# Nine of 32 rows of a graph convolution gathered by GpSimd between the packs of the other 23

## The chip, the core and the metric

The kernel runs on one NeuronCore of a Trainium2 chip. Its engines work side by side, each through its own stream of instructions in order: PE (TensorE, matrix products, with weight loads shown apart as PEld), DVE (VectorE), ACT (ScalarE), POOL (GpSimd, here the engine that issues gathers by index) and SP (SyncE, here only an issuer of plain DMAs). The metric is the device time of one execution in microseconds, as the median of several runs. Beside it there is one profiled execution, whose time is longer and whose rows carry the durations used below.

## What is computed

A graph has 12,500 nodes with 16 features each and 412,500 weighted edges, sorted by destination. Two stages follow each other. The first is a pair of graph convolutions, the second a mesh network with two message-passing steps over the same edges (64 features per edge), which the change does not touch. Each convolution does this:

```python
deg = segment_sum(ew, c)
dis = where(deg > 0, rsqrt(deg), 0)
norm = dis[r] * ew * dis[c]
msg = (x @ W.T)[r] * norm[:, None]
out = segment_sum(msg, c) + b
```

Here `r` is an edge's source and `c` its destination. So each edge fetches a row of 16 numbers by its source, multiplies it by a weight, and adds it into its destination. In the kernel the weight that is left at this place is `ew` alone: `dis` is multiplied into the table before and into the sums after, and the self-loops are put in when the table is made.

## The kernel before

**Rows.** The edges are cut into 128 rows of 3,223 (padded to `RL` = 3,328) in order of destination, so that a row covers fewer than `LR` = 112 destinations. A sort at the start (L204 to 361) orders each row by source. The key is source times 128 plus the destination's distance from the row's first node. From the sorted key come, for each edge, `mod` (the source modulo 256, bf16, written to HBM as `mod_d`), `slot_t` (which block of 256 sources, counted from the first of its tile's window), `drel_t` (the destination within the row) and `ew_t` (the weight). The last three are turned by PE (L347) so that 128 edges lie on the partitions and (tile, row) on the free axis. There are `NS` = 26 tiles of 128 edges in a row.

**The loop.** `messages` (L552) runs once per convolution. It makes the table of 12,500 rows of 16 numbers (`fill`), writes it to HBM (L558, L559), and holds it in SBUF as three bf16 parts `t3` whose sum is the fp32 value (`parts3`, L366). Then a hardware loop of `NR // RI` = 4 turns follows, with `RI` = 32 rows unrolled in each. All engines meet at the end of a turn. In a turn, for each row `r`:

- `load` (L575) has SP broadcast the row's `mod` to all partitions, 832 KB, one row ahead.
- `half_row` (L579) has DVE compare half of `mod` with the partition's number and with that number plus 128: two bf16 instructions of 1,664 elements, so four for a row. They are the one-hots `roh` that choose sources.
- `begin` (L587) has DVE make `wm`, the weight put at its slot, in two instructions, and takes a PSUM bank.
- `select` (L597) takes a pack of 4 or 5 tiles; a row has six packs. PE multiplies each tile's one-hots with `t3`, six bf16 matmuls a tile (three parts times two halves of 256), into a bank. DVE makes the one-hots of the destinations `ohd` (L611), then reads the bank times `wm` into `msg` (L614).
- `add_up` (L620) has PE sum `msg` over the pack's edges by `ohd`, in fp32, one pack behind; at a row's last pack ACT copies the sums out (L629).
- `fold_up` (L632) has PE sum the slots' sixteens (L635), and DVE adds the result to `agg` at the row's first node (L639).

**What sets the order.** The loop's code names no order beyond that of its text. A planner in the compiler's front end (the tile scheduler) lays every engine's stream out at build time. It walks a model of the machine with its own prices, and whenever an engine is free in that model it places an instruction that is ready there, the earliest of the text first. An instruction is ready when its inputs are done and its output has a buffer; each name of a tile has so many buffers (`bufs`, two if nothing is said; `roh`, `ohd` and `msg` have three). On the chip each engine then runs its stream strictly in that order and waits at semaphores. The later edge stage is different: there the streams of PE, DVE and ACT are kept in the text's order (`manual_schedule`), and POOL gathers eight times 128 rows of 64 numbers for each group of 1,024 edges (L415).

Of the kernel before, what the change touches and what calls it, by code (L numbers as in the profile page):

```python
# [29 lines left out]
SIGMAS = 4.5  # L30
LR = 112
RI = 32
EPS = 1e-5
MAGIC = 1597463007.0

# [2 lines left out]
def gcn_then_mesh_gnn_kernel(ctx: ExitStack, tc: tile.TileContext, a: dict, out: bass.AP):  # L38
# [86 lines left out]
    def bank(name):  # L125
        return psum.tile([128, 512], F32, name=f"ps_{name}")
# [77 lines left out]

    srt = ExitStack()
    so = srt.enter_context(tc.tile_pool(name="sorted", bufs=1))
    slot_t = so.tile([P, NS, NR], F32, name="slot_t")
    drel_t = so.tile([P, NS, NR], F32, name="drel_t")
    ew_t = so.tile([P, NS, NR], F32, name="ew_t")
    with tc.tile_pool(name="sort", bufs=1) as sp, \  # L210
            tc.tile_pool(name="psort", bufs=1, space=bass.MemoryType.PSUM) as pp:
        keys = [sp.tile([NR, RL], F32, name=f"key{i}") for i in range(2)]
# [90 lines left out]

        nc.vector.tensor_copy(ki, k)

        mod = sp.tile([NR, RL], BF16, name="mod")
        nc.vector.tensor_scalar(kj, ki, 7, 255, op0=OP.arith_shift_right, op1=OP.bitwise_and)
        nc.vector.tensor_copy(mod, kj)
# [31 lines left out]
        nc.vector.tensor_copy(k, ki)  # L340
        nc.sync.dma_start(rstat_d, st)
        for t, to in ((free, slot_t), (k, drel_t), (vals[turn], ew_t)):
            for j0 in range(0, NS, 4):
                n = min(4, NS - j0)
                pt = pp.tile([128, 512], F32, name="ps_st", bufs=2)
                for j in range(n):
                    nc.tensor.transpose(pt[:, j * NR:(j + 1) * NR], tiles(t)[:, j0 + j, :], ident)  # L347
                nc.scalar.copy(to[:, j0:j0 + n, :], pt[:, :n * NR].rearrange("e (j r) -> e j r", r=NR))
        rstat = sp.tile([1, 3, NR], F32, name="rstat")
        for i in range(3):  # L350
            nc.sync.dma_start(rstat[:, i, :], rstat_d[:, i:i + 1].rearrange("r o -> o r"))
# [153 lines left out]
    with tc.tile_pool(name="gcn", bufs=1) as gp, tc.tile_pool(name="gcnw", bufs=2) as gw:  # L505
# [7 lines left out]
            nc.sync.dma_start(fold[b * F:(b + 1) * F, :], ident[0:F, 0:F])  # L513
        iof = gp.tile([128, 2], F32, name="iof")
        nc.gpsimd.iota(iof, pattern=[[128, 2]], base=0, channel_multiplier=1, allow_small_or_imprecise_dtypes=True)
        ior = gp.tile([P, LR], F32, name="ior")
        nc.gpsimd.iota(ior, pattern=[[1, LR]], base=0, channel_multiplier=0, allow_small_or_imprecise_dtypes=True)
        xn = gp.tile([NP, NB, F], F32, name="xn")
        full, wide = N // P, 4 * P
        nwide = -(-N // wide)  # L520
# [31 lines left out]
        def messages(table, fill):  # L552
# [10 lines left out]
            with tc.tile_pool(name="rows", bufs=2) as rw:  # L563
                with tc.For_i(0, trip_count(2, NR // RI)) as it:
                    bases = rw.tile([1, RI], I32, name="rbases")
                    nc.vector.tensor_copy(bases, rbase_row[0:1, ds(it * RI, RI)])
                    mine = []
                    for t, name in ((slot_t, "rslot"), (drel_t, "rdrel"), (ew_t, "rew")):
                        c = rw.tile([P, NS, RI], F32, name=name, bufs=1)
                        nc.vector.tensor_copy(c, t[:, :, ds(it * RI, RI)])  # L570
                        mine.append(c)
                    slot, drel, ew = mine
                    rows, loaded, sums, folds = {}, {}, [], []

                    def load(r):  # L575
                        loaded[r] = rw.tile([128, RL], BF16, name="mod")
                        nc.sync.dma_start(loaded[r], mod_d[ds(it * RI + r, 1), :].to_broadcast([128, RL]))

                    def half_row(r, h):  # L579

                        oh = rw.tile([128, 2, RL // 2], BF16, name="roh", bufs=3)
                        for i in range(2):
                            nc.vector.tensor_scalar(oh[:, i, :], loaded[r][:, h * (RL // 2):(h + 1) * (RL // 2)],  # L583
                                                    iof[:, i:i + 1], None, op0=OP.is_equal)
                        return oh

                    def begin(r):  # L587
                        wm = rw.tile([P, NS, SB], F32, name="wm")
                        nc.vector.tensor_tensor(wm, iow[:, None, :SB].to_broadcast([P, NS, SB]),
                                                slot[:, :, r:r + 1].to_broadcast([P, NS, SB]), op=OP.is_equal)  # L590
                        nc.vector.tensor_tensor(wm, wm, ew[:, :, r:r + 1].to_broadcast([P, NS, SB]), op=OP.mult)
                        ohs = [None, None]
                        h = packs[0][0] // (NS // 2)
                        ohs[h] = half_row(r, h)
                        rows[r] = ohs, wm, bank("seg")

                    def select(r, j0, n, sb):  # L597
                        ohs, wm, acc = rows[r]
                        pg = bank("h")
                        for j in range(j0, j0 + n):  # L600
                            h, at = divmod(j, NS // 2)
                            if ohs[h] is None:
                                ohs[h] = half_row(r, h)
# [7 lines left out]
                        nc.vector.tensor_tensor(ohd[:, :n, :], ior[:, None, :].to_broadcast([P, n, LR]),  # L611
                                                drel[:, j0:j0 + n, r:r + 1].to_broadcast([P, n, LR]), op=OP.is_equal)
                        msg = rw.tile([P, 512], F32, name="msg", bufs=3)
                        nc.vector.tensor_tensor(  # L614
                            msg[:, :n * sb * F].rearrange("p (j s f) -> p j s f", s=sb, f=F),
                            pg[:, :n * sb * F].rearrange("p (j s f) -> p j s f", s=sb, f=F),
                            wm[:, j0:j0 + n, :sb, None].to_broadcast([P, n, sb, F]), op=OP.mult)
                        return r, j0, n, sb, ohd, msg

                    def add_up(r, j0, n, sb, ohd, msg):  # L620
                        acc = rows[r][2]
                        for j in range(n):
                            nc.tensor.matmul(acc[:sb * F, :LR], msg[:, j * sb * F:(j + 1) * sb * F],  # L623
                                             ohd[:, j, :], start=(j0 + j == packs[0][0]),
                                             stop=((j0, n, sb) == packs[-1] and j == n - 1))
                        if (j0, n, sb) == packs[-1]:
                            m = packs[0][2] * F
                            sl = rw.tile([SB * F, LR], F32, name="sl")
                            nc.scalar.copy(sl[:m], acc[:m, :LR])  # L629
                            folds.append((r, sl))  # L630

                    def fold_up(r, sl):  # L632
                        tot = bank("t")
                        m = packs[0][2] * F
                        nc.tensor.matmul(tot[:F, :LR], fold[:m], sl[:m], start=True, stop=True)  # L635
                        at = nc.values_load(bases[0:1, r:r + 1], engines=[ET.DVE], min_val=0, max_val=N,
                                            skip_runtime_bounds_check_because="a destination is a node's number or N")
                        w = agg[:, ds(at, LR)]
                        nc.vector.tensor_add(w, w, tot[:F, :LR])  # L639

                    load(0)
                    for r in range(RI):
                        if r + 1 < RI:
                            load(r + 1)
                        begin(r)
                        for i, pack in enumerate(packs):
                            sums.append(select(r, *pack))
                            if len(sums) > 1:
                                add_up(*sums.pop(0))
                            if folds and i >= 2:  # L650
                                fold_up(*folds.pop(0))
                    add_up(*sums.pop(0))
                    fold_up(*folds.pop(0))

        def spread_degrees():
            with tc.tile_pool(name="spread", bufs=2) as sw:
# [656 lines left out]
```

## Time and profile before

| | us |
|---|---|
| median of three runs (13,435.96 to 13,443.75) | 13,442.51 |
| the profiled execution | 15,403.32 |
| its span, first to last instruction | 15,401.6 |
| the first convolution's loop, four turns | 1,299 to 3,003 |
| the second convolution's loop, four turns | 3,131 to 4,836 |
| the two edge steps | about 5,120 to 15,350 |

The profile's page gives each engine's busy time, then the span cut into 40 slices of 385 us with the busy share of each engine in tenths. A second kind of view gives the busy time of each engine in a stretch. A third lists instructions in order of time with their duration and, in brackets, the idle time before them and what ended it. A fourth gives, for one tile, each instruction's shortest, median and longest duration in nanoseconds. Page groups that bear on the loop: PE at L607 (39,936 selecting matmuls) and L623 (13,312 records), DVE at L611, L614 and L583, and no POOL work at all.

### The profile page before, as it was taken

What the parts mean: (1) busy time and instruction counts of PE and PEld (TensorE: products, weight loads), DVE (VectorE), ACT (ScalarE), POOL (GpSimd) and SP (SyncE); (2) the same over time, 40 slices, a digit from 0 to 9 for tenths busy, and PEclk for the clock granted to TensorE, in tenths of its full rate; (3) what the DMA queues carried; (4) which work ended last, traced back from release to release, by engine and by line L of the source; (5) the groups of instructions that cost most, each with busy time, mean ns of one, the idle gap of its engine ahead of it and who ended that gap; (6) DMA issues with size and microseconds to landing.
All of it is one profiled execution on the core that took longest, in us unless ns stands there. A gap on an engine that the chain in (4) does not pass through costs nothing. (4 is left out here: it accounts for less than half of the span.)

```text
span 15401.6 us, 272960 instructions
## 1 busy us (share of the span) xinstructions
PE 11359.6 (74%) x104538; PEld 8563.0 (56%) x104539; DVE 8752.5 (57%) x22373; ACT 2374.3 (15%) x3731; POOL 6386.7 (41%) x6741
## 2 busy tenths in 40 slices
PE   0089999999998788888888888875666666666665
PEld 0078999889997455555555555553444444444443
DVE  9977777677777455455555555553444444444444
ACT  3400000000000222222222222221111111111111
POOL 0000000000001555556556665555666666666665
PEclk9999999999997688788888888886777777777777
DMA  0001111111111222222222222222222222222222
GB/s 29 0 15 54 66 64 66 50 67 66 65 65 47 56 59 59 58 60 62 59 59 62 59 62 60 60 60 59 61 60 60 61 60 60 61 60 60 61 59 50
DMA packets 958543, 871.49 MB, mean 57 GB/s; under 512 B 599416, under 2 KB 706192, under 8 KB 956548
## 3 DMA queue, kind: packets, MB, share of 16 engines
q1 hardware_dynamic: 258034, 493.54, 9.5%
q0 software_dynamic: 207360, 212.75, 6.8%
q10 hardware_dynamic: 491796, 147.08, 4.1%
q8 instruction: 859, 14.07, 0.4%
q14 instruction: 494, 4.05, 0.1%
HBM read 718.12 MB, written 134.51 MB: 55 GB/s over the span
## 5 line engine op out<-in xcount | busy, mean ns | idle before, releaser
L415 POOL DMA_INDIRECT pg<-tab_p,si x6480 | 6293.6, 971 | 3901.1 <-issue 1707.5
L1052 PE MATMUL ps_o<-eb_w,h 128*128 128x128 f32 x6480 | 1389.3, 381 | 1822.1 <-ACT h L1045 1623.5
L1052 PEld LDWEIGHTS ps_o<-eb_w,h 128*128 128x128 f32 x6480 | 1184.3, 274 | 2078.7 <-ACT h L1045 1762.4
L607 PE MATMUL ps_h<-t,roh 128*128 128x112 bf16 (+1 forms) x39936 | 2131.9, 211 | 65.9 <-DVE roh L583 65.9
L607 PEld LDWEIGHTS <-roh 128*128 128x128 bf16 x39936 | 2011.2, 98 | 115.3 <-issue 112.0
L789 POOL MEMSET zero<- 64x192 bf16 x1 | 0.3, 252 | 4015.1 <-DVE agg L639 4015.1
L1116 DVE TENSOR_SCALAR ot<-rb,iop 128x512 bf16<-128x512 bf16 x810 | 295.5, 365 | 2349.4 <-DMA rb<-relg_d 1482.8
L623 PE MATMUL ps_seg<-ohd,msg 128*112 128x112 f32 (+1 forms) x13312 | 1618.5, 266 | 0.0
L474 DVE TENSOR_REDUCE var<-sq 128x8 f32<-128x512 f32 (+2 forms) x1290 | 843.1, 666 | 1291.8 <-issue 743.9
L397 PE MATMUL ps_seg<-oh,y 128*64 128x64 f32 x19440 | 1298.7, 255 | 208.6 <-issue 197.9
L623 PEld LDWEIGHTS ps_seg<-ohd,msg 128*112 128x112 f32 (+1 forms) x13312 | 1407.4, 172 | 0.5
L397 PEld LDWEIGHTS ps_seg<-oh,y 128*64 128x64 f32 x19440 | 1141.8, 166 | 370.3 <-issue 348.0
L1040 PE MATMUL ps_h<-e,eb_w 128*128 128x512 f32 x1620 | 1193.3, 820 | 64.2 <-issue 36.4
L614 DVE TENSOR_TENSOR msg<-ps_h,wm 128x448 f32<-128x448 f32 (+1 forms) x1536 | 975.0, 635 | 460.5 <-PE ps_h L607 455.0
L611 DVE TENSOR_TENSOR ohd<-ior,rdrel 128x448 f32<-128x448 f32 (+1 forms) x1536 | 1011.1, 659 | 235.3 <-PE ps_seg L623 235.3
L473 ACT ACTIVATE sq<-ps_o 128x512 f32<-128x512 f32 (+1 forms) x1240 | 735.4, 593 | 2587.6 <-remote 668.8
L1045 ACT ACTIVATE h<-ps_h,eb_b 128x512 f32<-128x512 f32 x810 | 556.7, 687 | 3047.7 <-remote 2019.4
L1040 PE MATMUL ps_h<-ot,qd 128*128 128x512 bf16 x2430 | 784.4, 424 | 110.1 <-issue 97.3
L479 DVE TENSOR_TENSOR y<-ps_o,rs_y 128x512 f32<-128x512 f32 x1215 | 802.8, 688 | 88.1 <-issue 4.6
L385 DVE TENSOR_TENSOR oh<-iow,drl 128x512 f32<-128x512 f32 x1215 | 830.0, 683 | 14.4 <-DMA drl<-rel_d 7.2
L1042 PE MATMUL ps_h<-ident,pg 128*128 128x128 f32 x3240 | 603.1, 296 | 309.9 <-issue 236.5
L1052 PE MATMUL ps_o<-ee_w,h 128*128 128x128 f32 x3240 | 626.6, 353 | 238.5 <-ACT h L1033 232.8
(280 smaller groups left out, 11483.2 us busy)
## 6 DMA issues: line engine op xcount, KB each, us to landing
mod<-mod_d SPq DMA_DIRECT2D x256, 832.0 KB
pg<-tab_p,si POOLq DMA_INDIRECT x6480
e_d<-e SPq DMA_DIRECT2D x405, 256.0 KB
e<-e_d SPq DMA_DIRECT2D x405, 256.0 KB
rb<-relg_d ACTq DMA_DIRECT2D x1612, 64.0 KB
qd<-tab_q ACTq DMA_DIRECT2D x1612, 24.0 KB
at<-in_attrT SPq DMA_DIRECT2D x405, 32.0 KB
tab_q<-tabs SPq DMA_DIRECT2D x50, 187.5 KB
```

What stands on the lines that cost most here:

```text
L385: nc.vector.tensor_tensor(oh, iow[:, None, :].to_broadcast([P, K, W]), drl[:, g * K:(g + 1) * K, None].to_broadcast([P, K, W]), op=OP.is_e ...
L397: nc.tensor.matmul(ps[r:r + n, :W], v, oh[:, k, :], start=(k == 0), stop=(k == K - 1))
L415: nc.gpsimd.indirect_dma_start(out=to[:, k, :], out_offset=None, in_=table, in_offset=bass.IndirectOffsetOnAxis(ap=idx[:, k:k + 1], axis=0))
L473: nc.scalar.activation(sq, o.rearrange("p (k f) -> p k f", f=D), AF.Square, scale=D ** -0.5)
L474: nc.vector.tensor_reduce(v[:, i:i + k], sq, axis=AX.X, op=OP.add)
L479: nc.vector.tensor_tensor(y, o, r[:, i:i + k, None].to_broadcast(list(y.shape)), op=OP.mult)
L607: nc.tensor.matmul(pg[:, (j - j0) * sb * F:(j - j0 + 1) * sb * F], ohs[h][:, u, at * P:(at + 1) * P], t3[:, i, u, b:b + sb * F], start=(i ...
L611: nc.vector.tensor_tensor(ohd[:, :n, :], ior[:, None, :].to_broadcast([P, n, LR]), drel[:, j0:j0 + n, r:r + 1].to_broadcast([P, n, LR]), o ...
L614: nc.vector.tensor_tensor(msg[:, :n * sb * F].rearrange("p (j s f) -> p j s f", s=sb, f=F), pg[:, :n * sb * F].rearrange("p (j s f) -> p j ...
L623: nc.tensor.matmul(acc[:sb * F, :LR], msg[:, j * sb * F:(j + 1) * sb * F], ohd[:, j, :], start=(j0 + j == packs[0][0]), stop=((j0, n, sb) ...
L1040: nc.tensor.matmul(ph, w, v, start=(i == 0), stop=False)
L1052: nc.tensor.matmul(po[:, j * 128:(j + 1) * 128], h[:, j * P:(j + 1) * P], w1, start=False, stop=(j == KP - 1))
```

## The change

`GR = range(3, 28, 3)` names nine of the 32 rows of a turn. These rows no longer go through `load`, `half_row`, `begin`, `select`, `add_up` and `fold_up`. For each of them POOL fetches the 16 features of every edge's source from the table in HBM, 26 gathers of 128 rows (`fetch`, into `xg`, three buffers). DVE multiplies them by the weights and splits them into three bf16 parts `x3` (two buffers). DVE then makes one-hots of the destinations in bf16 for five tiles at a time (`goh`, two buffers), and PE sums each tile with one matmul of 48 columns, all 26 into one bank. ACT copies the bank, PE turns and adds the three parts with three small fp32 matmuls, and DVE adds the result to `agg`. The work of such a row is cut into ten pieces by a generator, and one piece is written behind each pack of the 23 other rows. The sources' numbers are kept for this as `src_t`, turned like the other three after the sort. `slot_t` and `drel_t` become bf16.

```diff
+GR = range(3, 28, 3)
...
-    slot_t = so.tile([P, NS, NR], F32, name="slot_t")
-    drel_t = so.tile([P, NS, NR], F32, name="drel_t")
+    slot_t = so.tile([P, NS, NR], BF16, name="slot_t")
+    drel_t = so.tile([P, NS, NR], BF16, name="drel_t")
+    src_t = so.tile([P, NS, NR // RI * len(GR)], I32, name="src_t")
...
+        nc.vector.tensor_single_scalar(kj, ki, 7, op=OP.arith_shift_right)
+        nc.vector.tensor_copy(vals[1 - turn], kj)
+        srcf = sp.tile([P, NS, NR // RI, len(GR)], F32, name="srcf")
+        turned_tiles(vals[1 - turn], lambda j0, n, v: nc.scalar.copy(
+            srcf[:, j0:j0 + n], v.rearrange("e j (i r) -> e j i r", r=RI)[:, :, :, GR.start:GR.stop:GR.step]))
+        nc.vector.tensor_copy(src_t, srcf.rearrange("e j i r -> e j (i r)"))
...
+                    srci = rw.tile([P, NS, len(GR)], I32, name="rsrc", bufs=1)
+                    nc.vector.tensor_copy(srci, src_t[:, :, ds(it * len(GR), len(GR))])
...
+                    def fetch(i):
+                        xg = rw.tile([P, NS, F], F32, name="xg", bufs=3)
+                        for j in range(NS):
+                            nc.gpsimd.indirect_dma_start(
+                                out=xg[:, j, :], out_offset=None, in_=table,
+                                in_offset=bass.IndirectOffsetOnAxis(ap=srci[:, j, i:i + 1], axis=0))
+                        return xg
+                    def gathered(i, xg):
+                        r = GR[i]
+                        x3 = rw.tile([P, NS, 3, F], BF16, name="x3")
+                        acc = bank("o")
+                        def weigh_row():
+                            nc.vector.tensor_tensor(xg, xg, ew[:, :, r:r + 1].to_broadcast([P, NS, F]), op=OP.mult)
+                        def split():
+                            parts3(rw, "x3", xg, [x3[:, :, k, :] for k in range(3)])
+                        def some(j0):
+                            n = min(5, NS - j0)
+                            oh = rw.tile([P, 5, P], BF16, name="goh")
+                            nc.vector.tensor_tensor(oh[:, :n, :], ior[:, None, :].to_broadcast([P, n, P]),
+                                                    drel[:, j0:j0 + n, r:r + 1].to_broadcast([P, n, P]), op=OP.is_equal)
+                            return lambda: [nc.tensor.matmul(
+                                acc[:, :3 * F], oh[:, j, :], x3[:, j0 + j].rearrange("p k f -> p (k f)"),
+                                start=(j0 + j == 0), stop=(j0 + j == NS - 1)) for j in range(n)]
...
+                        def turn(sl):
+                            tot = bank("t")
+                            for k in range(3):
+                                nc.tensor.matmul(tot[:F, :P], sl[:, k * F:(k + 1) * F], ident, start=(k == 0), stop=(k == 2))
...
+                            nc.vector.tensor_add(w, w, tot[:F, :LR])
+                        yield weigh_row()
+                        yield split()
+                        due = None
+                        for j0 in range(0, NS, 5):
+                            after = some(j0)
+                            if due:
+                                due()
+                            due = after
+                            yield
+                        due()
+                        sl = end()
+                        yield
+                        turn(sl)
+                    others = [r for r in range(RI) if r not in GR]
+                    due = {min(3 + (i * (len(others) - 3)) // (len(GR) - 1), len(others) - 1): i for i in range(len(GR))}
+                    fetched = {i: fetch(i) for i in range(2)}
+                    pieces = []
...
-                    load(0)
-                    for r in range(RI):
-                        if r + 1 < RI:
-                            load(r + 1)
+                    load(others[0])
+                    for m, r in enumerate(others):
+                        if m + 1 < len(others):
+                            load(others[m + 1])
+                        if m in due:
+                            i = due[m]
+                            pieces.append(gathered(i, fetched.pop(i)))
+                            if i + 2 < len(GR):
+                                fetched[i + 2] = fetch(i + 2)
                         begin(r)
                         for i, pack in enumerate(packs):
                             sums.append(select(r, *pack))
...
+                            piece()
                     add_up(*sums.pop(0))
                     fold_up(*folds.pop(0))
+                    while pieces:
+                        piece()
```

The gathered rows are thus written at the 4th, 6th, 9th, 11th, 14th, 16th, 19th, 21st and 23rd of the 23 other rows (`due` maps 3, 5, 8, 10, 13, 15, 18, 20, 22 to the gathered rows 0 to 8).

More of the change, by code (lines that the diff above doesn't have):

```diff
@@ L304, in gcn_then_mesh_gnn_kernel, with turned_tiles @@
         nc.vector.tensor_copy(ki, k)
+        def turned_tiles(t, put):
+            for j0 in range(0, NS, 4):
+                n = min(4, NS - j0)
+                pt = pp.tile([128, 512], F32, name="ps_st", bufs=2)
+                for j in range(n):
+                    nc.tensor.transpose(pt[:, j * NR:(j + 1) * NR], tiles(t)[:, j0 + j, :], ident)
+                put(j0, n, pt[:, :n * NR].rearrange("e (j r) -> e j r", r=NR))
+        nc.vector.tensor_single_scalar(kj, ki, 7, op=OP.arith_shift_right)
[4 more added lines that the diff above has]
+        nc.vector.tensor_copy(src_t, srcf.rearrange("e j i r -> e j (i r)"))
         mod = sp.tile([NR, RL], BF16, name="mod")
@@ L342, in gcn_then_mesh_gnn_kernel @@
         for t, to in ((free, slot_t), (k, drel_t), (vals[turn], ew_t)):
[L343 to L348, printed above, removed]
+            turned_tiles(t, lambda j0, n, v: nc.scalar.copy(to[:, j0:j0 + n, :], v))
         rstat = sp.tile([1, 3, NR], F32, name="rstat")
@@ L515, in gcn_then_mesh_gnn_kernel @@
         nc.gpsimd.iota(iof, pattern=[[128, 2]], base=0, channel_multiplier=1, allow_small_or_imprecise_dtypes=True)
-        ior = gp.tile([P, LR], F32, name="ior")
-        nc.gpsimd.iota(ior, pattern=[[1, LR]], base=0, channel_multiplier=0, allow_small_or_imprecise_dtypes=True)
+        ior = gp.tile([P, P], F32, name="ior")
+        nc.gpsimd.iota(ior, pattern=[[1, P]], base=0, channel_multiplier=0, allow_small_or_imprecise_dtypes=True)
         xn = gp.tile([NP, NB, F], F32, name="xn")
@@ L610, in select @@
                         ohd = rw.tile([P, 5, LR], F32, name="ohd", bufs=3)
-                        nc.vector.tensor_tensor(ohd[:, :n, :], ior[:, None, :].to_broadcast([P, n, LR]),
+                        nc.vector.tensor_tensor(ohd[:, :n, :], ior[:, None, :LR].to_broadcast([P, n, LR]),
                                                 drel[:, j0:j0 + n, r:r + 1].to_broadcast([P, n, LR]), op=OP.is_equal)
@@ new lines, in gathered, with end @@
+                    def gathered(i, xg):
[14 more added lines that the diff above has]
+                                start=(j0 + j == 0), stop=(j0 + j == NS - 1)) for j in range(n)]
+                        def end():
+                            sl = rw.tile([P, 3 * F], F32, name="gsl")
+                            nc.scalar.copy(sl, acc[:, :3 * F])
+                            return sl
+                        def turn(sl):
+                            tot = bank("t")
+                            for k in range(3):
+                                nc.tensor.matmul(tot[:F, :P], sl[:, k * F:(k + 1) * F], ident, start=(k == 0), stop=(k == 2))
+                            at = nc.values_load(bases[0:1, r:r + 1], engines=[ET.DVE], min_val=0, max_val=N,
+                                                skip_runtime_bounds_check_because="a destination is a node's number or N")
+                            w = agg[:, ds(at, LR)]
+                            nc.vector.tensor_add(w, w, tot[:F, :LR])
[12 more added lines that the diff above has]
+                        turn(sl)
@@ new lines, in messages, with piece @@
+                    others = [r for r in range(RI) if r not in GR]
+                    due = {min(3 + (i * (len(others) - 3)) // (len(GR) - 1), len(others) - 1): i for i in range(len(GR))}
+                    fetched = {i: fetch(i) for i in range(2)}
+                    pieces = []
+                    def piece():
+                        if pieces and next(pieces[0], 0) == 0:
+                            pieces.pop(0)
+                    load(others[0])
[7 more added lines that the diff above has]
+                                fetched[i + 2] = fetch(i + 2)
```

## The prediction

> **What bounds the kernel now.** I read the slices first, to find the stage that the change touches.
>
> ```profile
> PE   0089999999998788888888888875666666666665
> DVE  9977777677777455455555555553444444444444
> POOL 0000000000001555556556665555666666666665
> PEclk9999999999997688788888888886777777777777
> ```
>
> The two loops fill slices 3 to 12: PE at 9, DVE at 7, POOL at 0. Next the view of busy time by stretch, for one turn of the loop (columns: length; busy time and instructions of PE, PEld, DVE, ACT, POOL; granted clock; DMA share; GB/s).
>
> ```profile
> 2152.10:2578.70 426.60, 418.82 (x6720) 409.05 (x6720) 335.47 (x613) 8.09 (x32) 0.00 (x0) 0.99 0.18 66
> ```
>
> A turn lasts 426.6 us, PE is busy 98% of it at full clock, DVE 79%. The list in time order shows one row every 13.0 us (ACT copies a row's sums at 2007.28 and at 2020.29). So PE bounds this stage, 8 turns hold 3,413 us, DVE has 2.6 us spare a row and POOL is free. Then POOL's pace, from the edge stage, where gathers stand back to back:
>
> ```profile
> 8031.15 0.95 POOL L415 DMA_INDIRECT pg<-tab_p,si  x1 [0.31 <-issue]
> 8032.40 0.95 POOL L415 DMA_INDIRECT pg<-tab_p,si  x1 [0.30 <-issue]
> ...
> 8109.41 1.26 POOL L415 DMA_INDIRECT pg<-tab_p,si  x1 [2.07 <-remote]
> ```
>
> One starts every 1.25 us. Last, what lies on DVE at those moments, and how the planner fills a turn's start.
>
> ```profile
> 8032.39 0.34 DVE L1116 TENSOR_SCALAR ot<-rb,iop 128x512 bf16<-128x512 bf16 x1
> ...
> 8109.17 0.68 DVE L385 TENSOR_TENSOR oh<-iow,drl 128x512 f32<-128x512 f32 x1
> ...
> 2154.58 0.37 DVE L591 TENSOR_TENSOR wm<-wm,rew 128x208 f32<-128x208 f32 x1
> 2154.86 1.27 DVE L611 TENSOR_TENSOR ohd<-ior,rdrel 128x448 f32<-128x448 f32 x2
> 2156.05 0.37 DVE L589 TENSOR_TENSOR wm<-iow,rslot 128x208 f32<-128x208 f32 x1
> 2156.38 2.34 DVE L583 TENSOR_SCALAR roh<-mod,iof 128x1664 bf16<-128x1664 bf16 x4
> ...
> 1273.84 2.75 SPq L726 DMA_DIRECT2D dis<-dis_d  x6
> ...
> 3009.47 0.68 DVE L735 TENSOR_TENSOR t<-agg,dis 16x512 f32<-16x512 f32 x1 [6.05 <-issue]
> ```
>
> The second row's `wm` (2156.05) and the one-hots of later packs stand ahead of the first row's `roh`. Six loads of `dis` (as many as it has buffers) are issued at 1273.84, before a loop of four turns behind which they are first read, at 3009.47. So the planner moves work forward as far as buffers allow, whatever lies between in the text.
>
> **Removed.** Nine rows a turn at 13.0 us: 117 us of PE, with their DVE work and 832 KB loads.
>
> **Added, by engine, per gathered row.** PE: 26 matmuls with 128 bf16 weights; nearest row is L607, 24 pairs in 1.34 us, 0.056 each (48 moving columns here, 112 there): at most 1.5 us. The three fp32 products are like L635 (0.36 for two records): 0.5. Sum 2.0.
> DVE: fp32 products of two SBUF tensors take 369 ns at 208 elements, 619 at 448, 738 at 560, that is 150 + 1.04 per element. `weigh_row` (416) 0.59; two subtractions 1.17; three casts between the 294 ns (256 elements) and 568 (784) of `parts3` before, 0.38 each, 1.13; one-hots 5 x 0.82 (640) + 0.29 (128) = 4.39; the last add 0.26. Sum 7.5.
> POOL: 26 x 1.25 = 32.5 us, or 293 for nine, plus about 2 for the last to land (as the load of `d`, issued at 1265.71, is read at 1267.81).
>
> **Two parts of one rule, weighed.** The Trainium skill, SBUF — State Buffer, "Who interferes with whom", speaks against the change: a DVE instruction in a 2-port mode locks POOL out, so that its gathers starve. `roh` would be such (645 ns for 1,664 bf16, 353 for 512: 0.25 ns an element). By the rule 23 rows x 4 x 0.645 = 59 us a turn would be added to POOL, making 352. But the gather at 8032.40, started 0.01 us into an `ot` of this kind, took 0.95 like its neighbours. I take the trace: 0. The page's other half, that a DVE instruction with two SBUF inputs blocks a GpSimd one that reads SBUF, has its row: the gather at 8109.41 met `oh` and took 1.26, 0.31 more. In the loop `wm`, `ohd`, `goh` and the products are of that kind, half of DVE's time when it is busy. Bounds per gather: 0 to 0.3 us. I take 0.2 (POOL 339 a turn) where DVE is full, 0.05 (34 us a row) where it mostly waits.
>
> **In the text's order** this would pay. DVE has 10.4 us for an ordinary row; over the 1.67 rows that ten pieces span it has 17.4 + 7.5 = 24.9, PE 21.7 + 2.0 = 23.7. DVE leads slightly, and `split`, 2.3 us in one pack's 2.2, stalls PE once more by 1.5 or less. I take 4.2 us a gathered row: 23 x 13.0 + 9 x 4.2 + 12 (start, end) = 349; waiting for POOL's last row (339 + 4, then 1.67 rows) 365.
>
> **But the text's order isn't what runs.** `weigh_row` needs only `xg`, so the planner puts it on DVE wherever its model holds the gather done and DVE has a gap. On the chip DVE then stands at that place until the gather has landed, with every `ohd` and `msg` queued behind it, and PE, fed by those, stops too. What counts is where the planner believes 26 gathers to end. The trace of before has no gather in this loop; what I use is the order of the program as built, and only for places. In the convolution's spare gather loop (not run) the first product of eight gathers is placed behind 12 of them, the next behind 20. In the edge stage three DVE instructions of some 0.17 us stand between neighbouring gathers. So a gather is held to be worth about 0.5 us and 2 more to land: 15 us a row against 34 real. In our loop nine bf16 pairs stand beside a DVE instruction of 0.62 us, five beside one of 0.37: 0.07 a pair, so 156 pairs and 26 fp32 matmuls make a row of about 15, against 13.0 real. **The planner believes that one row of gathers takes one row of PE; it takes 2.6.**
>
> Places then, in rows from the turn's start. The first three `weigh_row` stand near 1.1, 2.1, 3.1, and not at 3, 5, 8. `xg` has three buffers, each freed by a `split`, and `x3` two, freed by the ninth piece of the row two before, whose matmuls do keep their place, as PE is full in the plan. That is row 4.5, 6.5, 9.5, 11.5 for `split` 2, 3, 4, 5. So `weigh_row` 3 to 5 stand near 4.1, 5.1, 6.1; gathers 6, 7, 8 start after `split` 3, 4, 5 and are expected a row later: 7.7, 10.7, 12.7.
>
> On the chip: gathers 0 to 5 run back to back and end at 2 + 6 x 34 + 2 = 208 us, with DVE at row 6.1 where PE could be after 90. `split` 3 follows half a row later (217), gather 6 ends at 253; 1.8 rows on `split` 4 (281; a row costs 14.6 with its share of pieces), gather 7 ends at 317; `split` 5 at 331, gather 8 at 367, with DVE at row 12.7. The 10.3 rows left take 150, end and barrier 7: **524 us a turn** against 426.6, 97.5 more, 780 over 8 turns. PE also cools in such waits: at a turn's start the clock is 0.60 in the stretch 2150 to 2160. That is about 2 us after each; most are covered by the next wait.
>
> **Small parts.** After the sort: shift and cast of 3,328 (about 2 us each by the 0.59 of an 832-element copy), 26 transposes with seven copies (L347's group of 52 records: 9.7), `src_t` 0.6, with DVE waiting: 15, or 5 if the planner fills it. Per turn one more copy and two bf16 sources: under 1 us, 6 in all. The table's write is issued 24 us before the loop, and the first gather waits behind it: 0. Together 20.
>
> **Sum.** +780 + 20 = +800 us. The execution profiled (15,403) would be 16,203. It is 1,961 over the median of the runs shown; the loop runs at clock 0.99 in it, the edge stage at 0.7 to 0.85, so I take the loop's microseconds as they are: 13,442 + 800 = **14,240**. If POOL is at 1.05 a gather without the profiler, a turn is near 467 (+340); with 0.15 more a gather than taken, near 550 (+1,000). The likeliest case's own range is 13,780 to 14,450.
>
> **Rivals.**
> 1. *The planner keeps the text's order* (or its price of a gather is near the real one, so that `weigh_row` stands at 2.2 rows a gather, which comes to the same). Turn 365, -61 x 8 + 20 = -470: **12,970**; with POOL off the path, 12,840. For it: PE is the bound and loses 117 us a turn. Against it: the rows at 2156.05 and 1273.84. From 427 us a turn it decides the sign: it needs `weigh_row` 8 behind about row 18.
> 2. *Half-way*: the planner moves pieces forward less than buffers allow, the last wait stands near row 17 to 18, and what PE saves is waited away: **13,450**. The same comes if gaps in DVE's plan are scarce.
> 3. *POOL is locked out after all* by `roh`, 0.25 us a gather on top: row 40 us, turn 575, **14,650**.
>
> The change could also do nothing if its loop weren't taken, but the trips are those of before.
>
> **How the numbers follow.** The likeliest case 0.62, rival 1 0.26, rival 2 0.08, rival 3 0.04. The predicted time is the likeliest's. The range takes that whole case, rival 2, and rival 1 down to 12,880. Within 0.2% (27 us, what a measurement can tell) is a third of rival 2, with the rest of it split: faster 0.29, same 0.03, slower 0.68.
>
> **What would show it.** Right: in the loop DVE's longest waits end with a landing of `xg` at `weigh_row`, nine a turn, most over 10 us; PE's share falls from 98% to about 60%, its clock below 0.95; turns of 480 to 550 us; POOL done at two thirds of a turn. Gathers lengthened beside `ohd`, not beside `roh`. Wrong: `weigh_row` found at its written row with no wait, turns of 350 to 370 and PE over 90%. The sum fails if a gather of 64 bytes has another pace than 1.25, or if PE places its 48-column matmuls early and frees `x3` sooner.

## The result, and the profile after

| | before | after |
|---|---|---|
| median of four runs each, us | 13,442.2 (13,435.96 to 13,443.75) | 14,355.33 (14,349.46 to 14,357.4) |
| ratio, 95% interval | | 1.068 [1.0661, 1.0698] |
| one turn of the convolution loop, us | 426.5 to 426.8 | 529.3 to 534.4 |

The changed kernel is slower by 913 us. Its profiled execution took 14,354.86 us, no longer than its median, so this profile shows the timed state of things. First its slices, to be held against those of before: POOL has gained work in slices 3 to 15, and PE there has fallen from 9 to between 5 and 7, with the clock at 7 and 8.

```profile
PE   0067656657567567888998889898677767767776
DVE  9986545645456457565766666666444444444444
POOL 0002454351643642477777777777677777777776
PEclk9998878877788788698999999999777777777777
```

The second view is one turn of the loop by stretch (columns as before: length, then busy time and instructions of PE, PEld, DVE, ACT, POOL, the granted clock, the DMA share, GB/s).

```profile
1841.10:2372.60 531.50, 334.58 (x5118) 321.91 (x5118) 294.23 (x558) 7.61 (x32) 242.49 (x234) 0.81 0.14 42
```

PE has 84 us less work than in a turn of before, and DVE 41 us less, yet the turn is 105 us longer. No engine is full: PE is busy 63% of the turn, DVE 55%, POOL 46%. So the turn is made of waits, and the next two views say which: the list of what DVE and PE waited for (us in all, times, longest), and the same moment in order of time.

```profile
DVE xg L675 <- DMA xg<-tab,rsrc: 1592.1, 72, 24.6
```

```profile
PE ps_seg L640 <- DVE msg L631: 1494.4, 72, 23.6
```

```profile
1879.97 0.59 DVE L675 TENSOR_TENSOR xg<-xg,rew 128x416 f32<-128x416 f32 x1 [24.29 <-DMA xg<-tab,rsrc]
1880.48 0.62 DVE L631 TENSOR_TENSOR msg<-ps_h,wm 128x448 f32<-128x448 f32 x1
```

```profile
1857.03 1.34 PE L624 MATMUL ps_h<-t,roh 128*128 128x112 bf16 x24
1881.15 1.84 PE L640 MATMUL ps_seg<-ohd,msg 128*112 128x112 f32 x8 [22.78 <-DVE msg L631]
```

All 72 `weigh_row` (nine in each of eight turns) found their gather unfinished, and DVE stood there for 199 us a turn. The first of this turn waited 24.29 us. The `msg` that PE needed was the very next instruction in DVE's stream; it ran half a microsecond after `weigh_row`, and PE, idle for 22.78 us, went on 0.7 us later. This is one chain: gather, `weigh_row`, `msg`, PE.

Where the other microseconds lie: the eight turns are 105.3 us longer each, 842 in all. The first turn starts at 1,309.6 us against 1,299, so the preparation cost 10.5. About 60 us remain, and lie behind the loops.

### The profile page after: what moved, and what is told of

It reads as the page before. It is cut to its first block, busy times and chain, and to the rows that moved or that the text cites. A ratio compares the mean times of both kernels' runs of the same rounds, so it can differ in the third digit from the quotient of the medians.

```text
span 14353.1 us, 247504 instructions
## 1 busy us (share of the span) xinstructions
PE 10061.7 (70%) x91139; PEld 7490.1 (52%) x91749; DVE 8401.7 (59%) x21952; ACT 2380.0 (17%) x3738; POOL 8294.6 (58%) x8613
## 5 line engine op out<-in xcount | busy, mean ns | idle before, releaser
L662 POOL DMA_INDIRECT xg<-tab,rsrc x1872 | 1929.1, 1031 | 2786.4 <-DVE wm L606 1657.7
L640 PE MATMUL ps_seg<-ohd,msg 128*112 128x112 f32 (+1 forms) x9568 | 1250.3, 279 | 1494.4 <-DVE msg L631 1494.4
L640 PEld LDWEIGHTS ps_seg<-ohd,msg 128*112 128x112 f32 (+1 forms) x9568 | 1089.8, 184 | 1505.8 <-DVE msg L631 1505.8
L624 PE MATMUL ps_h<-t,roh 128*128 128x112 bf16 (+1 forms) x28704 | 1605.3, 216 | 68.5 <-DVE roh L600 68.5
L624 PEld LDWEIGHTS <-roh 128*128 128x128 bf16 x28704 | 1489.0, 101 | 109.7 <-issue 104.0
L1146 PE MATMUL ps_o<-eb_w,h 128*128 128x128 f32 x6480 | 1245.7, 351 | 182.6 <-ACT h L1139 181.3
L1136 PEld LDWEIGHTS ps_h<-ident,pg 128*128 128x128 f32 x3240 | 442.0, 143 | 1695.2 <-issue 1235.5
L1146 PEld LDWEIGHTS ps_o<-eb_w,h 128*128 128x128 f32 x6480 | 1053.4, 247 | 440.3 <-ACT h L1139 310.5
L628 DVE TENSOR_TENSOR ohd<-ior,rdrel 128x448 f32<-128x448 f32 x1104 | 724.1, 656 | 110.0 <-PE ps_seg L640 107.6
L631 DVE TENSOR_TENSOR msg<-ps_h,wm 128x448 f32<-128x448 f32 x1104 | 694.5, 629 | 141.9 <-PE ps_h L624 138.4
```

The source lines that it names most:

```text
L662: nc.gpsimd.indirect_dma_start(out=xg[:, j, :], out_offset=None, in_=table, in_offset=bass.IndirectOffsetOnAxis(ap=srci[:, j, i:i + 1], ax ...
L1136: nc.tensor.matmul(ph[:, j * P:(j + 1) * P], pg[:, 2 * j:2 * j + 2, :].rearrange("p k f -> p (k f)"), ident, start=False, stop=(j == KP - ...
L1146: nc.tensor.matmul(po[:, j * 128:(j + 1) * 128], h[:, j * P:(j + 1) * P], w1, start=False, stop=(j == KP - 1))
```

## The experiments

All kernels of one group ran on one chip and are compared with the kernel before on that same chip. This matters here, because the chips differed: before took 13,434.6 us on one (as in the timed runs) and 15,388.9, 15,933.4 and 15,432.1 us on three others. Below these are "the chip of the timed kind" and "the other kind". The first profile, at 15,401.6 us, was by all signs taken on a chip of the other kind. It is not long because it was profiled: on such chips the runs of before that were not profiled take as long.

Two theories. **A, the prediction's:** the planner puts `weigh_row` where it believes the gathers are done, and DVE and PE stand there. **B, the rival:** gathers hold PE or DVE back by themselves, wherever `weigh_row` stands.

### First group, on a chip of the other kind (before: 15,388.94 us)

**The kernel before, for a trace.**

> The kernel before, profiled once more. If the 1,961 us by which its profiled execution exceeded its runs lay outside the convolutions' loops, the turns are again 426 to 427 us and the edge stage, 10.2 ms in the first profile, is 8.5 to 8.7 ms. If the loops are slower under the profiler too, the turns are near 372 (426.6 x 0.873).

Measured: 15,435.39 us with turns of 426.5 to 426.8 us. The loop runs as in the first profile, and the second group below shows the same turns on a chip of the timed kind. So the difference of some 2,000 us between the chips lies behind the loops, in the edge stage: 10,598 us here, against about 8,670 in the traces of changed programs from chips of the timed kind, where no trace of before was taken.

**weigh_row kept at its place in the text.** The built program then has it in rows 3.2, 5.2, 8.2 and so on to 22.2.

```diff
+                    newest = [None]
...
-                        nc.vector.tensor_tensor(
+                        newest[0] = nc.vector.tensor_tensor(
                             msg[:, :n * sb * F].rearrange("p (j s f) -> p j s f", s=sb, f=F),
...
-                        yield weigh_row()
+                        with tc.issue_after(newest[0].ins):
+                            weigh_row()
+                        yield
```

> The change with one edge more: weigh_row is not issued before the msg instruction that stands ahead of it in the text. Theory of the planner's order (DVE stands at a gather that the plan believes done, 12 rows too early): the waits at weigh_row vanish, a turn is 350 to 370 us, the time 12,850 to 13,000. Rival, the work itself is too dear (DVE's extra 7.5 us a row, gathers held up by DVE's instructions with two SBUF inputs): the waits move or become busy time, a turn stays over 427, the time over 13,440.

Measured: 16,491.68 us, ratio 1.0712 [1.0663, 1.0761], turns of 569 to 579 us. That speaks against theory A. No `weigh_row` waited for a gather any more, and yet the turn was some 146 us longer than before. The waits of PE in this run name no other engine:

```profile
PEld L625 <- issue: 1359.1, 1272, 17.1
```

PE started fewer instructions, and the profile names nothing that it waited for: 17 to 361 of them in 25 us with 18 gathers or more, against 810 in the median of 25 us with none.

**No gathers: POOL fills `xg` with zeros instead.** The nine rows' sources are left out, all other added work stays.

```diff
-                        for j in range(NS):
-                            nc.gpsimd.indirect_dma_start(
...
+                        nc.gpsimd.memset(xg, 0.0)
```

> Leaves out the 234 gathers of a turn (POOL sets xg to zero instead, so nine rows add nothing); all other added work stays, in nearly the planned order of the change. Theory of the planner's order: with nothing to wait for, early places harm nobody; a turn is 335 to 355, the time 12,700 to 12,900. Rival, the added DVE and PE work is what costs: a turn stays over 427, the time over 13,440.

Measured: 14,559.93 us, ratio 0.9466 [0.9408, 0.9525], turns of 324.2 to 324.7 us. One turn:

```profile
1700.00:2024.00 324.00, 315.33 (x5117) 304.56 (x5114) 293.77 (x560) 7.58 (x32) 4.35 (x9) 0.98 0.17 63
```

PE is at 97% and full clock again, with DVE at 91%. The arithmetic that the change adds is cheap, and the whole loss comes with the gathers: in the changed kernel, with them (on a chip of the timed kind), the same 5,118 matmuls took 531 us.

**Gathers alone.** All 32 rows go the old way, and the 234 gathers of a turn are issued but nobody reads them. `weigh_row` and the rest of the gathered rows' sums are left out.

```diff
-                    others = [r for r in range(RI) if r not in GR]
+                    others = list(range(RI))
...
-                            pieces.append(gathered(i, fetched.pop(i)))
+                            fetched.pop(i)
```

> All 32 rows go the old way; the 234 gathers of a turn are issued as well, into xg, and nobody reads them. Theory of the planner's order: gathers by themselves take nothing from PE or DVE; a turn is 427 to 431, the time within 13,440 to 13,520. Rival, POOL and DVE hold each other up (shared port): DVE's roh or ohd lengthen or start late, a turn is over 445, the time over 13,600. A gather takes 1.25 to 1.40 us from start to start beside a DVE that is 79% busy.

Measured: 17,813.7 us, ratio 1.1574 [1.1521, 1.1627], turns of 738 to 741 us. Two stretches of one turn, with gathers and without, and a few of its rows in order of time:

```profile
2055.00:2330.00 275.00, 32.91 (x141) 17.67 (x138) 6.42 (x10) 0.00 (x0) 209.48 (x216) 0.51 0.07 10
2420.00:2700.00 280.00, 280.00 (x4525) 273.56 (x4522) 223.79 (x409) 5.29 (x21) 0.00 (x0) 1.00 0.18 69
```

```profile
2106.88 0.95 POOL L662 DMA_INDIRECT xg<-tab,rsrc  x1 [0.31 <-issue]
2107.92 0.35 PE L640 MATMUL ps_seg<-ohd,msg 128*96 128x112 f32 x1 [2.46 <-issue]
2108.14 0.95 POOL L662 DMA_INDIRECT xg<-tab,rsrc  x1 [0.30 <-issue]
2109.32 0.23 PEld L640 LDWEIGHTS ps_seg<-ohd,msg 128*96 128x96 f32 x1 [2.57 <-issue]
2109.40 0.96 POOL L662 DMA_INDIRECT xg<-tab,rsrc  x1 [0.30 <-issue]
2110.66 0.95 POOL L662 DMA_INDIRECT xg<-tab,rsrc  x1 [0.30 <-issue]
2110.72 0.35 PE L640 MATMUL ps_seg<-ohd,msg 128*96 128x112 f32 x1 [2.45 <-issue]
```

While gathers stand back to back, PE starts one instruction every 1.40 us (a weight load at 2109.32, a matmul at 2110.72), although the profile names nothing that it waits for. In 275 us it ran 141 matmuls; without gathers it runs that many in 9. So B holds on this chip, and at once the question was whether it holds on the chip that was timed, where the trace of the changed kernel shows stretches of 14 us with PE at full speed beside gathers.

### Second group, on a chip of the timed kind (before: 13,434.58 us)

**The changed kernel itself.**

> The changed kernel itself, on the same chip as the three runs after it. Theory A (the planner's early weigh_row holds DVE, and PE behind it, until a row's gathers have landed): a turn of 529 to 534 us whatever the chip, before + 850 to 950 us. Theory B (the gathers hold back PE's issue of instructions, which the wait at weigh_row only hides): a turn of 530 to 580 us, with PE's idle time partly named issue rather than msg.

Measured: 14,343.98 us, ratio 1.0676 [1.0658, 1.0693], turns of 529.2 to 532.3 us, the same waits as above (1,597.4 us at `weigh_row`).

**weigh_row at its place in the text, again.**

> The changed kernel with weigh_row kept at its place in the text, a second time, beside the changed kernel. A: turns of 350 to 370 us, before - 450 to - 600 us. B: turns of 560 to 580 us as in the first run of it, before + 1,050 to + 1,250 us, with PE's idle time named issue and no weigh_row waiting for a gather. If the starvation belongs to the chip of the first run alone, this run goes to A's numbers on a chip where the kernel before takes 13,440 us.

Measured: 13,081.48 us, ratio 0.9738 [0.9722, 0.9754], turns of 369 to 375 us. The same program that lost 7% on the other chip gains 2.6% here, and beats both kernels. The waits of DVE, and one turn:

```profile
DVE xg L676 <- DMA xg<-tab,rsrc: 303.3, 36, 10.2
```

```profile
1683.90:2055.90 372.00, 326.35 (x5118) 313.86 (x5118) 295.34 (x560) 7.61 (x32) 278.32 (x234) 0.93 0.19 60
```

The waits at `weigh_row` fall from 1,597 us in 72 of them to 330 in 40 (303 of it ended by a landing), PE's share rises from 63% to 88%, and PE's weight loads for the selecting matmuls waited 109 us for issue in all eight turns, as good as in the changed kernel (104), against 1,359 on the other chip. Between this kernel and the changed one only the place of the nine `weigh_row`, and of what follows from them, differs: 1,262 us, or 158 a turn. On this chip A is shown.

Why 372 us and not fewer? In this run POOL was the bound. Its gathers stood without a pause from 2.7 to 352 us of the turn above, one every 1.49 us. Where DVE was full they lengthened, nine in a row at one place:

```profile
1807.81 1.67 POOL L663 DMA_INDIRECT xg<-tab,rsrc  x1 [0.30 <-issue]
1809.79 2.45 POOL L663 DMA_INDIRECT xg<-tab,rsrc  x1 [0.30 <-issue]
1812.54 2.41 POOL L663 DMA_INDIRECT xg<-tab,rsrc  x1 [0.30 <-issue]
```

The mean gather took 1.19 us, against 0.955 undisturbed. With the latter 234 of them would have ended at about 296 us (an estimate: 234 times 1.255, and 2.7).

**Half the gathers, unread.** All 32 rows as before; `xg` holds 13 tiles and `fetch` runs over `NS // 2`.

> All 32 rows as before, and 117 gathers a turn back to back (13 instead of 26 for each of nine rows), whose data nobody reads. A: no cost, turns of 427 to 431 us. B: a gather holds PE back by (738 - 427)/234 = 1.33 us, so 117 x 1.33 = 155 us, turns of 575 to 590 us, before + 1,180 to + 1,300 us; while the gathers run PE issues one instruction in 1.4 us.

Measured: 13,514.44 us, ratio 1.0059 [1.0043, 1.0076], with turns of 426.7 to 427.3 us:

```profile
1736.30:2163.10 426.80, 418.75 (x6720) 408.98 (x6720) 336.00 (x614) 8.09 (x32) 133.42 (x117) 0.99 0.20 68
```

117 gathers run back to back in the first 171 us of the turn, and PE's line is that of before to a tenth of a microsecond: 808 of its instructions in 25 us with 18 gathers or more, 807 with none (medians). On this chip gathers cost PE nothing, and B fails.

**The same gathers, spaced.** Four fills on POOL, of 517 ns in the mean, stand behind each gather, and a gather starts every 3.5 us.

```diff
+                            with tc.issue_after(g.ins):
+                                for _ in range(4):
+                                    m = nc.gpsimd.memset(pad, 0.0)
```

> As the run before (all rows as before, 117 unread gathers a turn), but with four fills of 533 ns on POOL behind each gather, so that one starts every 3.4 us instead of every 1.26. A: no cost, 427 to 431 us a turn. B with a price for each gather: 575 to 590 us as without the gaps. B with a price for their density (the gaps let PE fetch its instructions): 427 to 460 us a turn, before + 0 to + 270 us.

Measured: 13,517.1 us, ratio 1.0062 [1.0046, 1.0079], turns of 426.7 to 427.9. It tells nothing about the density of gathers, since here even dense ones are free. On a chip of the other kind it was not tried.

### Third group and last run, on two more chips of the other kind (before: 15,933.4 and 15,432.1 us)

**The kernel before, for a trace.** The aim was one from a chip of the timed kind, and the chip was not of it.

> The kernel before, for a trace of it from a chip where it takes about 13,440 us. Expected: turns of 426.6 us as in the first profile, so that the 1,961 us by which the first profile exceeds the median lie behind the loops: about 8,600 us from the end of the second loop to the end, against 10,565 in the first profile. The 80 us by which the runs with unread gathers (13,514 and 13,517 us) stand above before at equal turns: about 10 of them ahead of the first loop, the others where this trace is the shorter.

Measured: 15,900.02 us, turns of 426.4 to 426.8.

**Eight gathered rows, weigh_row at its place in the text.** `GR = range(3, 27, 3)`.

> weigh_row kept at its place in the text, and eight gathered rows instead of nine. With nine, a row's 26 gathers took 36 us and the places in the text come every 35 us, so every second weigh_row still waited, 303 us in all. With eight, the places come every three rows or 42 us, and no weigh_row should wait: a turn of 324 (without gathers) + 11.4 (one more row the old way) = 335 to 345 us, 12,770 to 12,870 us in all, 0.951 to 0.958 of before. If gathers slow PE even where nobody waits for them, more than 355 us a turn and no gain over the nine rows (13,081). On a chip where PE starves while gathers run, 540 to 570 us a turn instead.

Measured: 16,650.93 us, ratio 1.0443 [1.0393, 1.0494], turns of 550 to 554 us; PE's weight loads waited 1,295.4 us for issue. The last clause of the expectation came true, and the question it was made for stayed open.

**The preparation alone.** As the run with unread gathers, with a fill of `xg` in place of them; no gathered row is summed.

> What the change prepares (the sources' indices, slot and drel in bf16, the wider ior, the index copies in each turn), with all 32 rows as before; a fill on POOL stands in for each of the gathers, and no gathered row is summed. Turns of 427 us. If the 80 us of the runs with unread gathers belong to the preparation and to the program's layout: before + 60 to + 90 us. If the gathers cost them: before + 5 to + 20 us, the parts ahead of the loop alone.

Measured: 15,905.17 us, ratio 0.9982 [0.995, 1.0015], turns of 426.7 to 427.7. On this chip single runs spread over some 200 us, so 80 us can't be told from nothing.

**Eight rows, a second time.**

> Eight gathered rows, weigh_row at its place in the text, a second time. On a chip where before takes about 13,440 us: turns of 335 to 345 us with no or hardly any weigh_row waiting for a gather, 12,770 to 12,870 us in all, 0.951 to 0.958 of before; 372 us or more if a lower number of rows brings nothing. On a chip where before takes 15,400 us or more: turns of 545 to 560 us, as in its first run, with PE's idle time named issue.

Measured: 16,311.15 us, ratio 1.0545 [1.0504, 1.0587], turns of 548 to 551: again a chip of the other kind. Whether eight rows beat nine on a chip of the timed kind is not known; the 12,770 to 12,870 us expected there is an estimate.

### What the runs say together

| us a turn | timed kind | other kind |
|---|---|---|
| before | 426.7 (with unread gathers) | 426.5 |
| changed kernel | 531 | not run |
| weigh_row in the text's place | 372 | 569 to 579 |
| no gathers | not run | 324 |
| 234 unread gathers | 117 of them: 427 | 739 |

On the timed kind the account of a turn closes. Nine rows less save 102 us (324; measured on the other kind only, and taken over because the turns of before are the same on both). POOL's pace beside a busy DVE gives 48 back (372). The planner's places give back 159 more (531). The sum is +105.

## Why the prediction was right, and where its numbers were off

**The planner's places: right, and the cause on the timed chip.** In the built program `weigh_row` stands in rows 0.7, 1.7, 2.7, 3.7, 4.3, 5.8, 7.8, 10.8, 12.8; the prediction had 1.1, 2.1, 3.1, 4.1, 5.1, 6.1, 7.7, 10.7, 12.7. On the chip 0, 1, 2, 3, 4, 5, 7, 10 and 12 rows were done when they ran. Nine waits a turn, PE at 63% of it (60% forecast), clock 0.81 (below 0.95 forecast), a turn of 532 (480 to 550), gathers done at 385 us or 73% of a turn (two thirds).

**The turn, 524 forecast and 532 measured, from two errors against each other.** The last `weigh_row` ran at 387 us instead of 367, because a row of gathers took 34.6 us instead of 34 (26 times 1.33), and two of the nine waited longer for a buffer of `xg`: gathered row 5 stood 8.3 us where the sum had none, and row 6 some 16 where it had 11. The 11 rows then left took 12.8 us each (528 less 387, by 11), not 14.6 for 10.3 rows. Eight turns, each 7.9 us longer, make 63 us of the 115 by which 14,355 exceeds 14,240.

**The other 52.** The small parts ahead of the loops took 10.5 where the sum had 15 or 5. But the five traces of changed programs from chips of the timed kind spend 8,664 to 8,673 us behind the last row of the loops. Before spends about 8,600 there, worked out from its two medians less the 4,835 us at which its own traces reach that row. No term of the sum stood for this. The runs with unread gathers have it too, at unchanged turns. Its cause stays open.

**Added work on DVE and PE: mis-sized, on the safe side.** The single costs were right: `weigh_row` 592 ns (590 forecast), a cast 357 (380), a subtraction 592 (585), `goh` 4.37 us a row (4.39). What failed is the step from there to "DVE leads slightly", 4.2 us a gathered row. Without gathers the turn was 324, not 349: 1.5 us a gathered row, by 324 less 12 and 23 times 13.0, divided by nine. PE still bounds that loop, and its 2.0 us for such a row are about all that it costs.

**Rival 1 was priced well.** Its turn of 365 and total of 12,970 stand beside 372 and 13,081 for the kernel that does keep the text's order. Half of the 111 us between them is the 60 behind the loops.

**Gathers beside DVE: the size right, the split between its parts wrong.** The prediction took 0.2 us a gather where DVE is full and 0.05 where it mostly waits. Measured against the undisturbed 0.955: 0.19 in the run with half the gathers (1.14), 0.24 in the one that keeps the text's order (1.19), 0.08 in the changed kernel (1.03). But the prediction set `roh` at 0, and part of it comes from `roh`. Rows of the run with half the gathers in order of time, first POOL's and then DVE's:

```profile
1774.73 0.95 POOL L662 DMA_INDIRECT xg<-tab,rsrc  x1 [0.30 <-issue]
1775.99 2.03 POOL L662 DMA_INDIRECT xg<-tab,rsrc  x1 [0.30 <-issue]
```

```profile
1775.45 0.61 DVE L628 TENSOR_TENSOR ohd<-ior,rdrel 128x448 f32<-128x448 f32 x1
1775.99 1.20 DVE L600 TENSOR_SCALAR roh<-mod,iof 128x1664 bf16<-128x1664 bf16 x2
```

This gather began while an `ohd` was running; two `roh` followed that without a gap, and the gather took 1.08 us more. The one at 1762.99, with an `ohd` running and a single `roh` behind it, took 1.47. Others with `roh` beside them, such as the one at 1741.71, took 0.95. What decides is seen where the two kinds stand one by one (rows of POOL, `ohd` and `roh` alone):

```profile
1764.64 0.62 DVE L628 TENSOR_TENSOR ohd<-ior,rdrel 128x448 f32<-128x448 f32 x1 [0.34 <-PE ps_seg L640]
1764.76 1.34 POOL L662 DMA_INDIRECT xg<-tab,rsrc  x1 [0.30 <-issue]
1766.40 0.95 POOL L662 DMA_INDIRECT xg<-tab,rsrc  x1 [0.30 <-issue]
1766.82 0.62 DVE L628 TENSOR_TENSOR ohd<-ior,rdrel 128x448 f32<-128x448 f32 x1 [0.37 <-PE ps_seg L640]
1767.66 0.95 POOL L662 DMA_INDIRECT xg<-tab,rsrc  x1 [0.30 <-issue]
1768.54 0.65 DVE L600 TENSOR_SCALAR roh<-mod,iof 128x1664 bf16<-128x1664 bf16 x1
1768.91 1.10 POOL L662 DMA_INDIRECT xg<-tab,rsrc  x1 [0.30 <-issue]
```

The `ohd` that began 0.12 us before a gather cost it 0.39 us, the `roh` that began 0.37 us before one 0.15; the `ohd` that began 0.42 us after one cost nothing. In the run that keeps the text's order it is the same for the gathers with one `roh` or `ohd` and nothing else but `msg` beside them: 1.07 us in the mean where the `roh` had begun about 0.4 us earlier (24 gathers), 1.17 where the `ohd` had begun about 0.3 us earlier (39), and 0.95 to 0.96 in all 171 where an `ohd` began at least 0.2 us, or a `roh` at least 0.49 us, after the gather. So the Trainium skill's rule (SBUF — State Buffer, "Who interferes with whom": DVE in a 2-port mode locks POOL out) does bear on gathers, and the forecast "beside `ohd`, not beside `roh`" was half right. The prediction dismissed the rule by one `ot` that had begun 0.01 us before its gather; a `roh` so placed cost nothing either (nine gathers of 0.955 us with a `roh` begun within 0.07 us of their start).

**The profile and the median: the wrong explanation, harmless here.** I took the loop's microseconds as they are, which the runs bear out, but gave no cause for the 1,961 us. By the runs it was the chip: before takes 15,389 us in the median on another of this kind. POOL's own group in the edge stage shows where the time lies. First the kernel before in the first profile, whose row could be read ahead of the result, then the changed kernel on the timed kind, whose row could not (busy time and mean, then idle time ahead of the gathers):

```profile
L415 POOL DMA_INDIRECT pg<-tab_p,si x6480 | 6293.6, 971 | 3901.1 <-issue 1707.5
```

```profile
L430 POOL DMA_INDIRECT pg<-tab_p,si x6480 | 6272.3, 968 | 2038.2 <-issue 1236.6
```

The same 6,480 gathers, each as long as before, with 1,863 us more waiting between them. A profile that exceeds the median by 15% in the one stage where POOL gathers is a warning for a change that brings gathers elsewhere. That gathers might slow PE was in none of my cases. On the other kind of chip it decides, and that the timed chip was not of that kind was luck.

## What to carry to other kernels

A consumer that a planner may place freely will stand where the planner's prices put it; if it prices the producer too low, every engine behind that consumer pays. Look up the place in the built order, compare it with the real pace, and tie the consumer to an instruction that really runs that late: here this alone turned +6.8% into -2.6% on a chip of the timed kind. On the other kind the same kernel lost 7%, because gathers slowed PE. And when the profiled execution and the median differ, find the stage that makes the difference before using its rows.

## What the runs showed of the hardware that was not expected

On three of the four chips used for the experiments, PE started as few as 17 instructions in 25 us while POOL's gathers followed each other, and about 810 where none ran. With gathers back to back, one every 1.26 us, it was one instruction per 1.40 us. In that run PE's pace fell within some 15 us of a turn's first gather, and came back only 25 us after the end of the last. Between 13 and 340 us of such a turn one packet of 16,384 bytes came through the queue of instructions that keeps step with PE, where without gathers one came every 8 us. But 35 packets went with 9,047 instructions of PE in the 280 us without gathers, some 258 to a packet, and so many last 361 us at 1.40 us each. So the missing packets may be the effect and not the cause. With gathers spaced by their waits for a buffer the price was 1.06 us a gather (573 less 324, by 234), back to back 1.33 (738 less 427). On the fourth chip, of the timed kind, 117 gathers back to back cost PE nothing. What differs between the chips no run here shows; as each chip was used once, it may be the chip or a state that it was in.
